# A fused filter, bidirectional scan and FFN block: VectorE's side steps put on odd scans

## The chip, the cores and the metric

The kernel runs on one core of one Trainium2 chip. The metric is device microseconds of one execution, from launch to end; lower is better. Engines are named as in the profile: PE (TensorE matmuls, PEld its weight loads), DVE (VectorE), ACT (ScalarE), POOL (GpSimd) and SP (which issues the DMAs).

## The reference, cut to what matters

Eight images of 64 channels and 128 x 128 pixels go through two layers, all in float32.

1. **Filter.** A 3x3 convolution to 32 channels, a leaky ReLU and a 1x1 convolution give nine logits for each pixel. Their softmax is a low-pass kernel of that pixel; the output is `x + high`, where `high` sums nine shifted copies of x, each times (delta - softmax).
2. **Two bidirectional scans** (state space blocks) over the 16384 pixels of an image as one sequence. In short, for each direction and layer:

```
xc = silu(causal_conv1d(x));  dt = softplus(linear(xc));  B, C = linear(xc)
h[d,n,t] = exp(dt[d,t] * A[d,n]) * h[d,n,t-1] + dt[d,t] * B[n,t] * xc[d,t]      # 128 channels x 16 states
y[d,t]   = (sum over n of h[d,n,t] * C[n,t] + D[d] * xc[d,t]) * silu(z[d,t])
```

3. **Mix and FFN.** `x + dw * x_mamba`, where both factors are 3x3 convolutions (one per channel), then a layer norm, an FFN with a 3x3 convolution of 2 x 170 channels, gelu(g1) * g2, a projection and a residual sum.

## The kernel before, in words

**The scan is the backbone.** An image's sequence is cut into 16 time chunks of T = 1024, and it is walked four times (two layers, two directions), so an image has 64 chunks and the program 512. The channel-state pairs of a chunk (128 x 16 = 2048) fill 16 tiles of 128 partitions, so a chunk is **16 scans**, numbered u = 0 to 15 here, and the program has 8192 scans. Two neighbouring scans are a *pair* k (u = 2k and 2k+1). In each layer the second walk (`second`) also multiplies by the gate on DVE (`y_out`, L1272) and norms the result (`normed`, L1303); in the first walk ACT copies y out instead.

**One scan** is:
- `drive` (L1191, POOL, for a pair, written five scans ahead): bu = dt*x times B.
- `decay` (L1199, ACT, issued two scans ahead): w = exp(dt * A) into one of two PSUM tiles `w`.
- `scan` (L1218 or L1220, DVE): h = w*h + bu along time.
- `product` (L1235 DVE, L1237/L1239 POOL): h times C. For even u other than 4 and 12 it is POOL's (except in the scan after an FFN's gelu); then the scan writes to SBUF and its `w` tile is free when the scan ends. For odd u, and u = 4 and 12, it is DVE's own: the scan writes back into `w`, and that tile is free only when DVE's product has read it.
- `keep` (L1242, ACT): copies the last state for the next chunk.
- `collect` (L1257, PE): for a pair, sums over states into PSUM `y`.

**A chunk's preparation** runs beside the chunks before it: `conv` (L1066, PE, xp) and `conv_out` (L1072, ACT, xc) at u = 7 and 8, `gate` and `gate_out` (L1081, L1089) at 9 and 10, `silu` (L1092, ACT, with two table loads) at 11, `step`/`step_out` (L1108, L1115) at 14 and 15, `softplus` (L1121, ACT, with two table loads) at 2, `dtx` (L1147, POOL) at 5, and, for second walks, `project` (op, L1286), `residual` (L1292) and `square` (L1299) at 5 and 6.

**Beside the scans run the other layers of the next or the last image**, as tiles of 8 image rows: the *front* (filter, two layer norms, a root-mean-square norm; one tile each 24 scans), the *mix* (each 13) and the *FFN* (each 24). Seen from the start of an image's 1024 scans, the last image's mix takes about scan 0 to 174, its FFN 178 to 562, the next image's front 569 to 1010. Some tiles of the first and the last image run by other plans (`plan_alone`, and the `alone` branch of the FFN), which the change leaves as they are.

**What sets the order.** Nothing is left to a scheduler: `at(time, phase, function)` puts each step at a scan number and at one of seven phases within that scan, and the steps are written out in the order of (time, phase), within a phase in the order in which they were planned (chunks before tiles, older tiles before younger ones). Each engine then runs its own instructions strictly in that order.

```
    FEED, SCAN, MID, PROD, EXP, DECAY, REST = range(7)
            if u % 2 or u % 8 == 4 or self.t0 + u - 1 in gelu_times:
                return False
            return True
                at(b + u - 2, EXP, self.decay, u)
                at(b + u, SCAN, self.scan, u)
```

So DVE's side steps (`less_max`, `sums`, `weighted`, `scaled`, `third_norm` of the front, `times` and `scaled` of the mix, `rest_times` and `times` of the FFN), which are in phase MID, stand between that scan and, on odd u, DVE's own product. On an even u whose product is POOL's they stand between two scans. Steps of ACT's side are in DECAY, behind that scan's `keep` and `decay`; PE's, POOL's and SP's are in REST.

**Names that the change touches.** Front, with a = its start and b = a - 24: `logits` (lp, L547/L548), `less_max` (mx and lg, L554/L556), `exps` (L559, ACT), `sums` (sm, L563/L564), `softmax` (L567, POOL), three `piece` (sp, L571, ACT) and two `less_piece` (L575, POOL), `turn` (L580, PE) and `turned` (L584, ACT), nine `weight` (wb, L594, PE), `weighted` (t, L598, DVE) and `gather` (acc, L609, PE), `scaled` (hc, L629), `first_norm` (L633), `pointwise_out` (dwt, L642), `third_norm` (hn, L664). Mix: `times` (dwv, L820), `plus` (x, L823, POOL). FFN: `times` (ga, L961), `project` (fo, L972 to L977, PE), `add` (L983, ACT). Front tiles start alternately at u = 1 and u = 9 of a chunk, FFN tiles at u = 2 and u = 10; with 24 scans to a tile the pattern comes again every 48 scans, or three chunks. PSUM has one bank `bg`, one `acc`, one `mm` (xp, zp, dp, op) and one `y`.

## Time and profile before

| what | value |
|---|---|
| median of 3 runs | 28420.1 us (28417.24, 28420.1, 28466.43) |
| the profiled execution's own time | 28448.51 us |
| its span, first to last instruction | 28446.7 us |
| granted TensorE clock, mean | 0.881 |
| DVE busy | 26999.1 us (95%), 17438 instructions |
| POOL busy | 26718.7 us (94%), 8092 instructions |
| PE, ACT busy | 22906.5 us (81%), 18789.5 us (66%) |
| one DVE scan, one DVE product | 2343 ns, 1222 ns |
| one `drive`, one product on POOL | 4553 ns, about 2375 ns |
| `decay` on ACT | 1118 ns |

An engine's busy share is an average over stages. The table of windows and the timeline, which the prediction shows, tell which engine sets the pace in which stage; the view of waits names for each idle time the instruction that ended it. The profiled execution lies 28.4 us above the median of the three runs, inside their spread.

### The profile page before, as it was taken

Reading aid. Unit: us, or ns where it says so; the run is one execution under the profiler, and the core shown is the slowest. Engines: PE = TensorE matmul, PEld = TensorE weight load, DVE = VectorE, ACT = ScalarE, POOL = GpSimd, SP = SyncE. Lnnn points to the kernel's source line nnn. Section 1 sums busy time; section 2 is a strip of 40 time slices with the busy share of each in tenths; the row PEclk is TensorE's granted clock in tenths of the full one; section 3 lists DMA queues with packets and bytes.
Section 4 is the critical chain, followed back from the end, with each engine's and each line's share of the span. In section 5 each row is a group of like instructions: output and inputs, shape, how many; then the busy total and the mean of one; then the engine's idle time right before and its main releaser. Section 6 shows DMA issues by size and latency. Waiting matters only on the chain. (4 is left out here: it accounts for less than half of the span.)

```text
span 28446.7 us, 310539 instructions
## 1 busy us (share of the span) xinstructions
PE 22906.5 (81%) x97708; PEld 7249.4 (25%) x97708; DVE 26999.1 (95%) x17438; ACT 18789.5 (66%) x29130; POOL 26718.7 (94%) x8092
## 2 busy tenths in 40 slices
PE   7667888878888787888878788787887878888678
PEld 3212322223222232222322222222222222222123
DVE  6999999999999999999999999999999999999997
ACT  4666666666666666666666666666666666666663
POOL 4999999999999999999999999999999999999993
PEclk8777889988899888988889888898888988889789
DMA  6777787777877778777777777777777777777674
GB/s 163 233 243 226 239 259 244 243 231 237 263 245 241 228 241 262 241 241 230 246 256 242 239 232 248 254 246 235 234 252 246 250 229 239 255 244 248 209 257 138
DMA packets 2592492, 6762.70 MB, mean 238 GB/s; under 512 B 431494, under 2 KB 737046, under 8 KB 2589686
## 3 DMA queue, kind: packets, MB, share of 16 engines
q1 hardware_dynamic: 2589958, 6742.69, 73.0%
q8 instruction: 772, 12.65, 0.2%
q14 instruction: 882, 7.23, 0.1%
q10 hardware_dynamic: 880, 0.14, 0.0%
HBM read 5509.49 MB, written 1265.19 MB: 238 GB/s over the span
## 5 line engine op out<-in xcount | busy, mean ns | idle before, releaser
L1191 POOL TENSOR_TENSOR bu<-dup,bp 128x2048 f32<-128x2048 f32 x4096 | 18612.8, 4553 | 37.2 <-DMA bp<-bc_dram 17.9
L1199 ACT ACTIVATE w<-dtp,a_neg 128x1024 f32<-128x1024 f32 x8192 | 9162.7, 1118 | 1488.3 <-DVE hs L1220 657.6
L1235 DVE TENSOR_TENSOR hs<-w,cp 128x1024 f32<-128x1024 f32 x5232 | 6393.1, 1222 | 269.3 <-DMA cp<-bc_dram 99.1
L1220 DVE TENSOR_TENSOR_SCAN w<-w,state,bu 128x1024 f32<-128x1024 f32 x2651 | 6212.1, 2343 | 155.2 <-ACT w L1199 126.0
L1218 DVE TENSOR_TENSOR_SCAN w<-w,state,bu 128x1024 f32<-128x1024 f32 x2581 | 6048.4, 2343 | 95.8 <-ACT w L1199 75.1
L1257 PE MATMUL y<-hs,sel_y 128*32 128x512 f32 x32768 | 4996.0, 688 | 748.9 <-POOL hs L1239 434.2
L1242 ACT COPY state<-w 128x1 f32<-128x1 f32 x5232 | 828.5, 158 | 5315.9 <-DVE hs L1235 5253.4
L1237 POOL TENSOR_TENSOR hs<-hs,cp 128x1024 f32<-128x1024 f32 x1515 | 3609.4, 2382 | 332.8 <-DVE hs L1218 217.6
L1239 POOL TENSOR_TENSOR hs<-hs,cp 128x1024 f32<-128x1024 f32 x1445 | 3423.4, 2369 | 423.8 <-DVE hs L1220 299.4
L1218 DVE TENSOR_TENSOR_SCAN hs<-w,state,bu 128x1024 f32<-128x1024 f32 x1515 | 3550.2, 2343 | 155.3 <-ACT state L1242 74.5
L1220 DVE TENSOR_TENSOR_SCAN hs<-w,state,bu 128x1024 f32<-128x1024 f32 x1445 | 3384.5, 2342 | 97.9 <-ACT state L1242 61.9
L1066 PE MATMUL xp<-hn,wx 128*128 128x512 f32 x4096 | 2459.4, 731 | 1036.6 <-ACT xc L1072 434.2
L897 PE MATMUL fp<-fw,bgw 128*128 128x512 f32 (+1 forms) x5760 | 2166.7, 622 | 166.3 <-DMA fw<-xn_dram 166.0
L1108 PE MATMUL dp<-xc,wdt 128*128 128x512 f32 x2048 | 1356.2, 749 | 635.6 <-ACT dt L1115 305.9
L1257 PEld LDWEIGHTS y<-hs,sel_y 128*32 128x32 f32 x32768 | 720.6, 114 | 4456.2 <-issue 2557.1
L1250 PE MATMUL y<-xc,dskip 128*64 128x512 f32 x4096 | 1381.2, 759 | 404.4 <-ACT yv L1274 302.5
L1072 ACT ACTIVATE xc<-xp,cbias 128x512 f32<-128x512 f32 x1024 | 701.3, 685 | 1195.0 <-PE xp L1066 1191.0
L1066 PEld LDWEIGHTS xp<-hn,wx 128*128 128x128 f32 x4096 | 839.6, 224 | 2524.4 <-issue 1033.7
L68 ACT ACT_TABLE_LOAD x1137 | 1458.8, 1283 | 21.3 <-PEq L1429 0.7
L903 PE MATMUL fp<-fw,bgw 64*128 64x512 f32 (+1 forms) x5760 | 1385.7, 608 | 0.0
L609 PE MATMUL acc<-t,ident 128*128 128x512 f32 x2160 | 1307.1, 693 | 0.0
L594 PE MATMUL wb<-wt,sel_k 65*128 65x512 bf16 x1152 | 509.4, 443 | 979.6 <-DVE t L598 975.5
(212 smaller groups left out, 25989.6 us busy)
## 6 DMA issues: line engine op xcount, KB each, us to landing
bp<-bc_dram SPq DMA_DIRECT2D x4096, 256.0 KB, 4.0
dup<-du_dram SPq DMA_DIRECT2D x4096, 256.0 KB, 5.2
dtp<-dt_dram SPq DMA_DIRECT2D x4096, 256.0 KB, 5.1
cp<-bc_dram SPq DMA_DIRECT2D x4096, 256.0 KB, 4.8
hn<-hn_dram SPq DMA_DIRECT2D x1024, 256.5 KB, 4.4
dt_dram<-dt SPq DMA_DIRECT2D x512, 512.0 KB, 3.0
du_dram<-du SPq DMA_DIRECT2D x512, 512.0 KB, 2.6
yf_dram<-yv SPq DMA_DIRECT2D x512, 256.0 KB, 3.3
```

What stands on the lines that cost most here:

```text
L68: nc.scalar.preload_act_table_set("natural_log_exp_and_others")
L897: nc.tensor.matmul(o, wpair[:, i, g, m], self.win[h][:, i : i + ROWS, 0:W], start=(i == 0), stop=False)
L903: nc.tensor.matmul(o, wlast[rows, i, g, m], self.win[h][rows, i : i + ROWS, lo : W + lo], start=False, stop=(i == 2),)
L1066: nc.tensor.matmul(self.xp[h], wx[:, self.l, self.d, i, :], self.hn2[:, s.start + 2 * i : s.stop + 2 * i], start=(i == 0), stop=(i == 1),)
L1191: nc.gpsimd.tensor_tensor(bu, self.dup[self.pairs[k][1]], self.over_pair("bp", k), ALU.mult)
L1199: nc.scalar.activation(w, self.dtp[gp][:, i, :], AF.Exp, scale=a_neg[:, self.l, self.d, g, j : j + 1])
L1218: nc.vector.tensor_tensor_scan(to, w, bu, s0, ALU.mult, ALU.add)
L1220: nc.vector.tensor_tensor_scan(to[:, ::-1], w[:, ::-1], bu[:, ::-1], s0, ALU.mult, ALU.add)
L1235: nc.vector.tensor_tensor(out, hs, c, ALU.mult)
L1237: nc.gpsimd.tensor_tensor(out, hs, c, ALU.mult)
L1239: nc.gpsimd.tensor_tensor(out[:, ::-1], hs[:, ::-1], c[:, ::-1], ALU.mult)
L1257: nc.tensor.matmul(self.y[lo : lo + 32, :], sel_y, hs[:, i, s], start=False, stop=(k % 4 == 3))
```

## The change

All edits are to the numbers of the plan; no instruction is added or taken away.

- **Front.** `less_max` goes from scan a - 1 to a (and from phase DECAY to MID), `exps` with it; `sums` and `softmax` from a + 1 to a + 2; the pieces, `turn` and `turned` one scan later; `gather` one later; both `scaled` and all that hangs on them (`first_norm`, `pointwise`, `pointwise_out`, the second centring, `second_norm`, the stores) one later; `third_norm` from a + 55 to a + 56. As a is odd, all of DVE's moved steps go from even to odd scans. The nine `weighted` stay.
- **Mix.** `times`, `plus`, `scaled` and `norm` go to the next odd scan where they were on an even one.
- **FFN.** The two `times` of a tile go from one even scan (a + 20) to the odd ones at a + 19 and a + 21; `load_x2`, `project`, `add` and the store go one scan later.
- **Scan.** `collect` of the pairs k = 1 and k = 5 goes one scan later (u = 6 and 14).
- One `load_hn` (that of chunk 14) goes one scan later.

```diff
-            at(b + 23, DECAY, self.less_max)
-            at(b + 23, DECAY, self.exps)
-            at(b + 25, MID, self.sums)
-            at(b + 25, REST, self.softmax)
+            at(a, MID, self.less_max)
+            at(a, DECAY, self.exps)
+            at(a + 2, MID, self.sums)
+            at(a + 2, REST, self.softmax)
             for i in range(3):
-                at(b + 26 + 2 * i, DECAY, self.piece, i)
+                at(a + 3 + 2 * i, DECAY, self.piece, i)
                 if i < 2:
-                    at(b + 27 + 2 * i, REST, self.less_piece, i)
-            at(b + 31, REST, self.turn)
-            at(b + 32, DECAY, self.turned)
+                    at(a + 4 + 2 * i, REST, self.less_piece, i)
+            at(a + 8, REST, self.turn)
+            at(a + 9, DECAY, self.turned)
...
-                at(t + 13, REST, self.gather, k)
+                at(a + k + 14, REST, self.gather, k)
...
-            at(a + 29, MID, self.scaled, n1)
-            at(a + 29, DECAY, self.first_norm)
-            at(a + 30, REST, self.pointwise)
-            at(a + 31, DECAY, self.pointwise_out)
+            at(a + 30, MID, self.scaled, n1)
+            at(a + 30, DECAY, self.first_norm)
+            at(a + 31, REST, self.pointwise)
+            at(a + 32, DECAY, self.pointwise_out)
...
-            at(a + 37, MID, self.scaled, n2)
-            at(a + 37, DECAY, self.second_norm)
-            at(a + 37, REST, self.store_h)
-            late, end = (a + 46, a + 55) if self.c < NCH - 1 else (a + 37, a + 43)
+            at(a + 38, MID, self.scaled, n2)
+            at(a + 38, DECAY, self.second_norm)
+            at(a + 38, REST, self.store_h)
+            late, end = (a + 46, a + 56) if self.c < NCH - 1 else (a + 38, a + 44)
...
-            at(a + 8, MID, self.times)
-            at(a + 8, REST, self.plus)
+            at(a + 8 | 1, MID, self.times)
+            at(a + 8 | 1, REST, self.plus)
...
-            at(a + 17, MID, self.scaled, n1)
+            at(a + 17 | 1, MID, self.scaled, n1)
...
-                groups = ((0, 0, self.first_out, 5), (6, 2, None, 0), (14, 1, self.times, 20))
-                gelus, out = GELU, 20
+                groups = ((0, 0, self.first_out, 5), (6, 2, None, 0), (14, 1, self.times, 19))
+                gelus, out = GELU, 21
...
-                    at(a + to, MID if end == self.times else DECAY, end, h)
+                    late = 0 if self.alone or end == self.first_out else 2 * h
+                    at(a + to + late, MID if end == self.times else DECAY, end, h)
...
-            at(b + (5 if self.i == NCH - 2 else 3), REST, self.load_hn)
+            at(b + (6 if self.i == NCH - 2 else 3), REST, self.load_hn)
...
-                at(b + 2 * k + 3 + (k % 4 == 0), REST, self.collect, k)
+                at(b + 2 * k + 3 + (k % 4 < 2), REST, self.collect, k)
```

More of the change, by code (lines that the diff above doesn't have):

```diff
@@ L678, in plan @@
             at(b + 21, REST, self.logits)
-            at(b + 23, DECAY, self.less_max)
-            at(b + 23, DECAY, self.exps)
-            at(b + 25, MID, self.sums)
-            at(b + 25, REST, self.softmax)
+            at(a, MID, self.less_max)
+            at(a, DECAY, self.exps)
+            at(a + 2, MID, self.sums)
+            at(a + 2, REST, self.softmax)
             for i in range(3):
-                at(b + 26 + 2 * i, DECAY, self.piece, i)
+                at(a + 3 + 2 * i, DECAY, self.piece, i)
                 if i < 2:
-                    at(b + 27 + 2 * i, REST, self.less_piece, i)
-            at(b + 31, REST, self.turn)
-            at(b + 32, DECAY, self.turned)
+                    at(a + 4 + 2 * i, REST, self.less_piece, i)
+            at(a + 8, REST, self.turn)
+            at(a + 9, DECAY, self.turned)
             at(a + 6, REST, self.load_xb)
             for k in range(9):
-                t = a + k
-                at(t + 11, DECAY, self.weight, k)
-                at(t + 12, MID, self.weighted, k)
-                at(t + 13, REST, self.gather, k)
+                at(a + k + 11, DECAY, self.weight, k)
+                at(a + k + 12, MID, self.weighted, k)
+                at(a + k + 14, REST, self.gather, k)
             at(a + 23, DECAY, self.filtered)
@@ L702, in plan @@
             at(a + 27, REST, n1.spread, bg_tile)
-            at(a + 29, MID, self.scaled, n1)
-            at(a + 29, DECAY, self.first_norm)
-            at(a + 30, REST, self.pointwise)
-            at(a + 31, DECAY, self.pointwise_out)
-            at(a + 31, REST, self.store_rows, dw_img[self.p], "dwt")
-            at(a + 31, REST, self.centered, acc_tile, "xn")
-            at(a + 32, DECAY, self.centered_out)
-            at(a + 33, REST, lambda: n2.means(acc_tile, self.sq))
-            at(a + 34, DECAY, n2.means_out)
-            at(a + 35, REST, n2.spread, acc_tile)
-            at(a + 37, MID, self.scaled, n2)
-            at(a + 37, DECAY, self.second_norm)
-            at(a + 37, REST, self.store_h)
-            late, end = (a + 46, a + 55) if self.c < NCH - 1 else (a + 37, a + 43)
+            at(a + 30, MID, self.scaled, n1)
+            at(a + 30, DECAY, self.first_norm)
+            at(a + 31, REST, self.pointwise)
+            at(a + 32, DECAY, self.pointwise_out)
+            at(a + 32, REST, self.store_rows, dw_img[self.p], "dwt")
+            at(a + 32, REST, self.centered, acc_tile, "xn")
+            at(a + 33, DECAY, self.centered_out)
+            at(a + 34, REST, lambda: n2.means(acc_tile, self.sq))
+            at(a + 35, DECAY, n2.means_out)
+            at(a + 36, REST, n2.spread, acc_tile)
+            at(a + 38, MID, self.scaled, n2)
+            at(a + 38, DECAY, self.second_norm)
+            at(a + 38, REST, self.store_h)
+            late, end = (a + 46, a + 56) if self.c < NCH - 1 else (a + 38, a + 44)
             at(late, DECAY, self.third_square)
@@ L850, in plan @@
             at(a + 15, REST, n1.spread, bg_tile)
-            at(a + 17, MID, self.scaled, n1)
-            at(a + 17, DECAY, self.norm)
-            at(a + 17, REST, self.store_rows, xn_img, "hc")
+            at(a + 17 | 1, MID, self.scaled, n1)
+            at(a + 17 | 1, DECAY, self.norm)
+            at(a + 17 | 1, REST, self.store_rows, xn_img, "hc")
     def plan_mix(b, a, step):
```

## The prediction, made before the changed kernel had run

> **What bounds the kernel now.** I read the page first (DVE 95% busy, POOL 94%), then the windows by stage, then DVE's waits, then timelines of single chunks; the order of both programs' instructions shows what moves where. Below, four windows in the middle of the run: mix and early FFN, late FFN, and the front in first and in second walks. Columns: window, busy us of PE, PEld, DVE, ACT, POOL, granted clock, DMA share, GB/s.

> ```profile
> 7298.60:8140.30 841.70, 666.04 (x2842) 181.30 (x2840) 802.28 (x460) 560.13 (x840) 841.70 (x251) 0.89 0.79 254
> 8140.30:9004.80 864.50, 758.40 (x3155) 236.39 (x3151) 832.71 (x507) 592.43 (x880) 813.66 (x231) 0.96 0.74 246
> 9261.50:9855.20 593.70, 461.97 (x2009) 150.87 (x2009) 582.42 (x401) 403.00 (x653) 584.76 (x192) 0.86 0.69 227
> 9855.20:10623.30 768.10, 650.18 (x2965) 238.42 (x2963) 740.51 (x529) 529.78 (x873) 710.63 (x227) 0.88 0.73 236
> ```

> In the first window POOL is busy for all of its 841.70 us: POOL sets the pace for the first quarter of each image, and what DVE saves there buys nothing. In the others DVE is idle for 11 to 32 us and POOL for 9 to 57: DVE sets the pace, less its stalls. So the change can win two things: cheaper side steps, and fewer stalls.

> **Term 1: a side step is cheaper on an odd scan.** DVE's timeline in a front chunk:

> ```profile
> 10143.77 2.34 DVE L1218 TENSOR_TENSOR_SCAN hs<-w,state,bu 128x1024 f32<-128x1024 f32 x1
> 10146.03 0.66 DVE L598 TENSOR_TENSOR t<-xb,wb 128x512 f32<-128x512 f32 x1
> 10146.61 2.35 DVE L1218 TENSOR_TENSOR_SCAN w<-w,state,bu 128x1024 f32<-128x1024 f32 x1
> ...
> 10155.76 2.35 DVE L1218 TENSOR_TENSOR_SCAN w<-w,state,bu 128x1024 f32<-128x1024 f32 x1
> 10158.02 0.67 DVE L598 TENSOR_TENSOR t<-xb,wb 128x512 f32<-128x512 f32 x1
> 10158.61 1.21 DVE L1235 TENSOR_TENSOR hs<-w,cp 128x1024 f32<-128x1024 f32 x1
> 10159.73 2.34 DVE L1218 TENSOR_TENSOR_SCAN hs<-w,state,bu 128x1024 f32<-128x1024 f32 x1
> 10161.99 2.33 DVE L1218 TENSOR_TENSOR_SCAN w<-w,state,bu 128x1024 f32<-128x1024 f32 x1
> 10164.35 1.23 DVE L1235 TENSOR_TENSOR hs<-w,cp 128x1024 f32<-128x1024 f32 x1
> 10165.50 2.34 DVE L1218 TENSOR_TENSOR_SCAN hs<-w,state,bu 128x1024 f32<-128x1024 f32 x1
> ```

> From start to start, an even scan takes 2.26 us bare (10159.73 to 10161.99) and 2.84 with a side step (10143.77 to 10146.61): 0.58 for the step. An odd scan with its product takes 3.51 bare (10161.99 to 10165.50) and 3.97 with a step in between (10155.76 to 10159.73): 0.46. Independent instructions overlap by some 0.08 us, while the product that needs its scan starts 0.03 after the scan's end; a side step fills that hole. Saved: 0.12 us for each step that stood alone and stands alone again. [...] The 2.36 us (scan to its product) against 2.26 (scan to an independent step) above show a difference here, and I follow the rows.

> - Front, 120 tiles (7 x 16 + 8): three lone groups each (mx with lg, the first hc, hn) go to odd scans where nothing stands: 360 x 0.12 = 43 us. The second hc stands beside a t before and after: 0. sm falls beside yv in second walks, and in first walks just ahead of a scan that waits for softplus: 0. Half of the mx groups (60) fall in chunks whose scans 10 and 11 wait for ACT anyhow: minus 7. Left: 36.
> - FFN, 112 tiles: two steps in one even scan (2 x 0.58) become two lone ones (2 x 0.46): 0.24 x 112 = 27; the first fifth of the FFN lies in POOL's stretch: 21.
> - Mix: POOL's stretch, 0; at most some 125 steps x 0.12 = 15.

> **Term 2: a stall filled in the FFN.** In the second walk, chunk type 1 (chunk number mod 3), scan 14 waits 0.43 us for ACT, behind silu (30 times in six images, 13.0 us), and both `times` stand behind it. With the first at scan 13 the wait shrinks by its 0.43: x 6 x 7 images = 18 us.

> **Term 3: PE's order in the FFN.** The largest single stall of DVE in the FFN:

> ```profile
> 8432.91 1.98 PE L972 MATMUL fo<-ga,bgw 128*64 128x512 f32 x4
> ...
> 8437.95 1.98 PE L1066 MATMUL xp<-hn,wx 128*128 128x512 f32 x4
> 8439.98 0.69 ACT L1072 ACTIVATE xc<-xp,cbias 128x512 f32<-128x512 f32 x1 [4.88 <-PE xp L1066]
> ...
> 8442.38 2.36 DVE L1220 TENSOR_TENSOR_SCAN w<-w,state,bu 128x1024 f32<-128x1024 f32 x1 [2.67 <-ACT w L1199]
> ```

> The FFN's projection (fo, 4.1 us here) stands between the two halves of xp; ACT waits 4.88 us for the second half with the next `decay` behind it, and scan 11 starts 2.67 us late. This is so in chunk type 0 of second walks, 18 times in six images, 49.7 us. With `project` one scan later, fo stands behind the second xp in PE's order. That xp could start once xc's first half is out (8433.74) and, at the 3.78 us that the first half took at half clock, end at 8437.6; xc then ends at 8438.3 and `decay` at 8439.7, against 8439.63 as scan 11's earliest start: no stall. 49.7 x 7/6 = 58 us; I take 50, since fo now stands ahead of zp, and ACT's gate copy can cost up to 0.4 us in each of the 21 chunks. Bounds 0 and 58.

> **Term 4: ACT's steps ahead of silu (u = 11) in the front.** Scan 14 there waits 62 us in six images. One sp cast (0.23 us; chunk type 2) and one pair of r steps (0.26 + 0.21; type 1) go from 11 to 12, behind the `decay` that is late: 0.23 x 8 x 7 = 13 and 0.42 x 4 x 7 = 12. Of these 25 I take 20; bounds 0 and 25.

> **Term 5, a cost: ACT's steps ahead of softplus (u = 2).** `pointwise_out` (0.68 us) goes from u = 0 to u = 1 in chunk type 0, into ACT's unbroken run from `keep` to `decay(5)`. In first walks scan 5 has 0.03 us to spare there (median): 0.65 x 3 x 7 = 14 us lost. In second walks 1.3 us to spare hides it; without that cover 24 more (bounds 0 and 38).

> **Term 6, a cost: POOL's order.** POOL's timeline at the first front tile of an image:

> ```profile
> 5814.96 0.30 POOL L567 TENSOR_TENSOR lg<-lg,sm 128x72 f32<-128x72 f32 x1
> 5815.22 2.35 POOL L1239 TENSOR_TENSOR hs<-hs,cp 128x1024 f32<-128x1024 f32 x1
> 5817.54 4.54 POOL L1191 TENSOR_TENSOR bu<-dup,bp 128x2048 f32<-128x2048 f32 x1
> ```

> `softmax` now comes behind this product and `drive`: 5821.8 to 5822.1. ACT's first sp cast, one scan later than before, then stands in front of `keep` and `decay` of scan 7, which is done at 5823.7; scan 7 started at 5822.63 and would start 0.23 earlier now: 1.3 us lost. `less_piece` comes behind dtx and one more `drive`, at 5829.2; the next cast, with hidden_out's 1.3 us behind it, delays scan 9 by 2.8. Together about 4.2 us an image, 29 for seven. Stalls let POOL catch up: at scan 6 it starts its product 7 to 8 us behind the scan's end here, but 3.1 in the median first-walk chunk and at most 2.6 in second walks, and the cast hurts only from about 3 us on. I take 30; bounds 0 and 60.

> **Term 7: lp.** mx waits for PE at u = 8 (28.8 us in six images, 34 in seven), and one scan later it won't. But that PE queue (project, lp, xp) holds ACT, too: scans 10 and 11 there wait 52 us, and the time would reappear there, or at sm, which now waits for `exps` behind a gate copy. I take 0; bounds minus 20 and plus 34.

> **At nothing.** The third norm's means (PE) now wait for lg of one scan later, as both use bank bg: about 2.5 us of PE's queue once a tile, hidden because ACT reaches the result 1.5 us after it is done; uncovered, some 1 us x 100. POOL's waits for sm and sp (41 and 71 us in the front) vanish: POOL has room there. `gather` and `collect` one later free PE of waits for POOL (62 us in the front) and are needed by nothing sooner. The next FFN tile's first matmul finds bank bg free one scan after `add` is due, not two: its result is due five scans later. SP's queue moves with its producers: loads lead their use by two scans or more.

> **Sum.** 36 + 21 + 18 + 50 + 20 - 14 - 30 + 0 = 101 us. Against the profiled execution's own 28448.5 us: 28347. The median of the runs is 28420, so this is 0.26% below it; 0.2%, about 57 us, is what a measurement of this kernel can tell from no change (28363 and 28477).

> **Rivals.**
> 1. *Slower: POOL's order decides in every front tile.* Without term 6 the sum is 131 us; over 120 front tiles a stall of 1.1 us each takes all of it, and from 1.6 us on the kernel is slower. For it: in first walks POOL's lag of 3.1 us is just at the margin, and cheaper side steps in the same stretch (u = 1 to 9) raise it. Against: second walks, and that a stall cures the lag. At 2 us each: 28448.5 - 131 + 240 = 28557.
> 2. *No change: the stalls move.* ACT and PE are in order, and what one chunk's scan 11 gains another wait takes back (term 3 at half or less, 4 at nothing, 5 and 6 as above): 36 + 21 + 0 + 12 - 14 - 30 = 25, so 28424.
> 3. *The change doesn't do what it says.* The order listing shows the steps ahead of the products and fo behind xp: excluded.

> **Chances and range.** The forecast (a gain beyond 57 us) 0.62, no change 0.20, slower 0.18. All terms at their best: 43 + 42 + 18 + 58 + 25 + 34 = 220, 28228; three runs reach 31 us below the profiled execution, so I go to 28215. At the worst bounds (half of term 3, no 2 and 4, 14 + 60 + 20 lost): 12 us over the old, 28460; a part of the slower rival takes it to 28490.

> **What would show it.** Right: odd scans with a lone step at 3.97 us; fo behind the second xp and no wait near 2.7 us at scan 11; DVE's busy time as before and its idle time some 60 to 100 us smaller. Wrong: ACT waiting for lg on POOL for several us, with DVE waiting for `decay` at scans 7 and 9; waits for sm on ACT; POOL's idle time growing in the first quarter of an image.

## The result, and the profile after

The changed kernel takes 28604.8 us (median of 6 runs, 28584.99 to 28622.85) against 28421.8 us for the kernel before (6 runs beside it): a ratio of 1.0060, 95% interval 1.0050 to 1.0071. By the ratio it is about 170 us slower (the two medians lie 183 us apart), where 101 us less were forecast. Its profiled execution took 28590.2 us, with a span of 28588.4 us.

Busy time by engine, from the top of the page of the changed kernel:

```profile
span 28588.4 us, 310543 instructions
PE 23060.4 (81%) x97708; PEld 7247.1 (25%) x97708; DVE 26930.1 (94%) x17438; ACT 18772.1 (66%) x29130; POOL 26719.2 (93%) x8092
```

DVE is busy 69 us less than before (26999.1), with the same number of instructions: the cheaper side steps are there. But the span grew by 142 us, so DVE is idle for some 211 us more. PE is busy 154 us *more* (22906.5 before) for the same 97708 matmuls, and the mean granted clock fell from 0.881 to 0.874. They ran slower; hold on to that.

The same four windows as in the prediction, cut at the same scans of the same image (us; busy PE, PEld, DVE, ACT, POOL; granted clock, DMA share, GB/s):

```profile
7389.10:8234.20 845.10, 666.75 (x2847) 181.85 (x2846) 800.45 (x460) 558.98 (x840) 843.53 (x252) 0.88 0.78 251
8234.20:9077.70 843.50, 742.06 (x3154) 228.52 (x3150) 828.84 (x506) 594.40 (x880) 811.00 (x230) 0.98 0.76 253
9333.80:9936.90 603.10, 472.25 (x1989) 154.16 (x1991) 579.99 (x402) 400.90 (x652) 584.74 (x191) 0.83 0.68 223
9936.90:10718.90 782.00, 671.73 (x2987) 244.57 (x2980) 738.55 (x529) 528.26 (x872) 710.80 (x228) 0.86 0.71 232
```

The late FFN takes 843.5 us instead of 864.5. Both front windows grew, 593.7 to 603.1 and 768.1 to 782.0, though DVE is busy 2 us less in each, and the granted clock in them fell from 0.86 to 0.83 and from 0.88 to 0.86. Over the whole run, from scan to scan, the FFN of seven images (scans 176 to 592) gains 109 us. The front of seven (592 to 984) loses 169, image 0's front 35, and the 216 scans between front and FFN, with the front's last steps and the mix, lose 30. These are single executions. A stage that no edit touches differs by some 30 us from one profile to another (the FFN of the kernel with S alone, below), so smaller differences of a stage show little.

What DVE waited for (waits of DVE; us in total, times, longest):

```profile
DVE w L1217 <- ACT w L1198: 240.2, 202, 2.5
DVE hs L1217 <- ACT w L1198: 171.7, 113, 8.0
DVE w L1219 <- ACT w L1198: 159.8, 125, 2.8
```

Before, these three read:

```profile
DVE w L1218 <- ACT w L1199: 75.1, 105, 2.3
DVE hs L1218 <- ACT w L1199: 70.0, 47, 3.0
DVE w L1220 <- ACT w L1199: 126.0, 96, 2.8
```

Scans that wait for `decay` on ACT account for 300 us of new waiting, more than the whole 211. Of the other waits some grew (`normed` for its spread by 33 us, `times` of the FFN by 27) and some fell. Adding up DVE's idle time ahead of scans, products, `t` and `mx` by chunk type (six images, as in the prediction), front stalls went from 206 to 381 us. Where they stand is in the table below.

Terms 1 and 3 are to be seen as forecast. DVE's timeline in a front chunk, with a lone `hc` on an odd scan:

```profile
10278.36 2.35 DVE L1217 TENSOR_TENSOR_SCAN hs<-w,state,bu 128x1024 f32<-128x1024 f32 x1 [0.85 <-ACT w L1198]
10280.62 2.33 DVE L1217 TENSOR_TENSOR_SCAN w<-w,state,bu 128x1024 f32<-128x1024 f32 x1
10282.86 0.67 DVE L629 TENSOR_TENSOR hc<-hc,rb 128x512 f32<-128x512 f32 x1
10283.45 1.21 DVE L1234 TENSOR_TENSOR hs<-w,cp 128x1024 f32<-128x1024 f32 x1
10284.58 2.34 DVE L1217 TENSOR_TENSOR_SCAN hs<-w,state,bu 128x1024 f32<-128x1024 f32 x1
```

From 10280.62 to 10284.58 it is 3.96 us, where 3.97 was expected. In the FFN, the chunk that answers to the one shown before:

```profile
8525.46 1.98 PE L1065 MATMUL xp<-hn,wx 128*128 128x512 f32 x4
8527.37 1.08 PE L970 MATMUL fo<-ga,bgw 128*64 128x512 f32 x4
8527.48 0.69 ACT L1071 ACTIVATE xc<-xp,cbias 128x512 f32<-128x512 f32 x1 [1.41 <-PE xp L1065]
...
8530.59 2.33 DVE L1219 TENSOR_TENSOR_SCAN w<-w,state,bu 128x1024 f32<-128x1024 f32 x1
```

`fo` stands behind the second xp, ACT waits 1.41 instead of 4.88 us, and scan 11 starts without a wait.

### The profile page after: what moved, and what is told of

The parts are those of the page before. It is cut to its first block, busy times and chain, and to the rows that moved or that the text cites. A ratio compares the mean times of both kernels' runs of the same rounds, so it can differ in the third digit from the quotient of the medians.

```text
span 28588.4 us, 310543 instructions
## 1 busy us (share of the span) xinstructions
PE 23060.4 (81%) x97708; PEld 7247.1 (25%) x97708; DVE 26930.1 (94%) x17438; ACT 18772.1 (66%) x29130; POOL 26719.2 (93%) x8092
## 5 line engine op out<-in xcount | busy, mean ns | idle before, releaser
L1256 PE MATMUL y<-hs,sel_y 128*32 128x512 f32 x32768 | 5059.5, 693 | 378.8 <-POOL hs L1238 311.7
```

What stands on the lines that cost most here:

```text
L1256: nc.tensor.matmul(self.y[lo : lo + 32, :], sel_y, hs[:, i, s], start=False, stop=(k % 4 == 3))
```

## The experiments

The change falls into parts that can be put in or taken out alone: F, the FFN's two edits; S, the softmax chain (mx to `turned`) a scan later; N, the two norm chains, pointwise and gather a scan later; C, the sums over states of pairs 1 and 5 a scan later. Each kernel was compared with the kernel before on the same chip; a ratio of 0.001 is 28 us. The mix's moves were not tried alone: over scans 0 to 176 of seven images the nine kernels with them are -1 to 14 us longer than the kernel before, the six others -1 to 9, so no effect of theirs can be seen.

### One part back, or one part alone

**F alone.** The kernel before with these lines of the diff, shortened:

```
-  (14, 1, self.times, 20))        gelus, out = GELU, 20
+  (14, 1, self.times, 19))        gelus, out = GELU, 21
+  late = 0 if self.alone or end == self.first_out else 2 * h
```

> The kernel before with the FFN's edits alone (times at 19 and 21, project and add one scan later). Theory A (the prediction's FFN terms hold, the loss is made elsewhere): terms 1, 2 and 3 of the FFN give 21 + 18 + 50 = 89 us less than the kernel before, about 28331; scan 11 of chunk type 0 in second walks no longer waits 49.7 us in six images. Rival B (the FFN's edits are part of the loss, because fo now holds zp or the wait at ga grows): 28420 or more.

Measured: 0.9984 (0.9976 to 0.9993), 45 us faster. Theory A in direction, half in size (see term 2 below). The loss is elsewhere.

**One part taken out of the changed kernel**: C (`(k % 4 < 2)` back to `(k % 4 == 0)`), S (the lines mx to `turned` back to `b + 23` ... `b + 32`), N (`a + 30` ... `a + 38` back to `a + 29` ... `a + 37`, `end` to `a + 55`, gather to `a + k + 13`).

> The changed kernel with only the sums over states put back (pairs 1 and 5 of each chunk at scans 5 and 13 again). Theory C: in the front those matmuls, a scan later, stand on PE ahead of the second dp (asked for at scan 15) and of op and xp (scans 5 to 8), so that bc comes 1 to 2 us later and decay(3) with it; putting them back gives most of the 38 us of scan 3's waits and a part of those at scans 10 and 11: 60 to 100 us less than the changed kernel's 28605. Rival D (the loss is from the front's own steps): within 25 us of 28605.

> The changed kernel with only the softmax chain of the front (mx, lg, exps, sums, softmax, pieces, turn) put back one scan earlier. Theory S: exps behind the gate copy and sm waiting for it on DVE in chunk type 2, POOL's softmax behind drive, and the casts behind POOL are the loss at scans 7, 9, 10 and 11: the waits there shrink by 29 + 66 - 29 (mx waits again) us in six images, so some 80 us less than 28605. Rival D2 (norm chain or sums over states): within 25 us of 28605.

> The changed kernel with the front's two norm chains (with pointwise, the third norm's end) and gather put back one scan earlier. Theory N: second_norm at scan 15 behind the second dt and pointwise_out at scan 1 ahead of softplus lie in ACT's unbroken stretch up to decay(5), and cost the waits of scans 3 and 5 (0 to 38 us and 10 to 43 us in six images, before and after): 70 to 100 us less than 28605, even though term 1's 0.12 us a step for two of three lone groups (24 us) is given up. Rival D3 (it is the softmax chain or the sums over states): 28605 or a little more.

Measured: C back 1.0023 (1.0013 to 1.0033), S back 1.0017 (1.0008 to 1.0026), N back 1.0006 (0.9997 to 1.0015). Against the 1.0060 of the change, the parts put back return 105, 122 and 154 us. All three gave back more than their theories said (60 to 100, some 80, 70 to 100), and together they would return 381 us of a loss of 216 (171 plus the 45 of F). The parts are not independent.

**One part put into the kernel before**, nothing else:

> The kernel before with only pairs 1 and 5 of each chunk's sums over states a scan later. Theory I (shared slack: each part is hidden while the other two stand where they were, so the costs do more than add): within 30 us of the kernel before, since the FFN wins some 35 us by it (84 against 50 in its late part with and without) and the front loses about 25 to 45. Rival J (each part costs what its undoing gave back): some 90 us slower than before.

> The kernel before with only the softmax chain of the front (mx to turn) one scan later. Theory I: 30 to 50 us slower: the 29 us of mx's wait at scan 8 reappear at scan 10, and POOL's late softmax and pieces cost about 28 us in six images at scans 7, 9 and 11 of chunk type 1. Rival J: some 110 us slower. The prediction's terms 1, 6 and 7 for this part alone: 36/3 + 0 - 30, so about 18 us slower.

> The kernel before with only the front's norm chains, pointwise, third norm's end and gather one scan later (and the one load of hn that has to follow). Theory I: 50 to 80 us slower, from scan 5 of chunk type 0 (term 5 of the prediction, there minus 14), scan 3 of type 1 and scan 11 of type 2. Rival J: some 140 us slower. The prediction's own terms for this part: 24 (two of three lone groups) + 12 - 14, so 20 us faster.

Measured: C 1.0017 (1.0008 to 1.0025), S 1.0013 (1.0004 to 1.0022), N 1.0017 (1.0008 to 1.0026): 48, 37 and 48 us slower. With F's -45 that adds up to 88 us; the change costs 171. In size theory I holds for S and, just below its range, for N; C was expected within 30 us and is at 48, and its profile places it where the theory did (front 55 us longer, FFN 26 shorter). For S and N the profiles do not: their steady front stretches are as long as before (0 and -3 us), and S alone shows 34 us in the FFN, none of whose steps it moves. Where S and N alone lose their time is thus not shown. All parts together lose 169 us in the front. So the question became: what is harmless there alone and costs when two come together?

### Where the parts meet: PE's order and its clock

The stalls of DVE in the front, us in six images ("type" is the chunk number mod 3, counted from the start of the image):

| place | before | change | C back | S back | N back | gather | turn | filler | PE order |
|---|---|---|---|---|---|---|---|---|---|
| scan 5, type 0 | 2 | 33 | 33 | 22 | 2 | 30 | 31 | 26 | 31 |
| t at scans 8, 9, type 0 | 34 | 30 | 0 | 47 | 62 | 66 | 45 | 41 | 0 |
| scan 3, type 1 | 0 | 38 | 16 | 12 | 0 | 2 | 32 | 19 | 0 |
| scans 7, 9, 11, type 1, first walks | 0 | 29 | 31 | 0 | 28 | 32 | 31 | 28 | 29 |
| scans 13, 14, type 1, second walks | 10 | 37 | 51 | 0 | 10 | 49 | 10 | 18 | 10 |
| mx, scans 10, 11, type 2, second walks | 81 | 117 | 124 | 84 | 94 | 104 | 106 | 113 | 98 |
| scan 11, type 2, first walks | 10 | 40 | 31 | 16 | 20 | 14 | 37 | 43 | 8 |
| all ahead of scans, products, `t`, `mx` | 206 | 381 | 347 | 267 | 273 | 353 | 355 | 359 | 236 |

(The last row leaves out the waits of `sm`: 39 us with S back, some 11 in the others, 2 before.)

Scans 13 and 14 show the meeting most clearly: 10 us or less without S or without N, 37 to 51 with both (the change, C back, gather). Here is one such chunk of the changed kernel (timeline of PE, ACT and DVE; in brackets the idle time before and who ended it):

```profile
10552.07 0.69 ACT L642 ACTIVATE dwt<-dwp,v_dw_b 128x512 f32<-128x512 f32 x1
...
10552.81 2.07 PE L621 MATMUL cp<-hc,center 128*128 128x512 f32 x2 [1.77 <-ACT dwt L642]
...
10554.81 0.63 PE L580 MATMUL tp<-identb,sp 128*54 128x128 bf16 x4
...
10555.37 1.97 PE L1080 MATMUL zp<-hn,wz 64*64 64x512 f32 x4
...
10557.38 0.58 ACT L1088 COPY gate<-zp 128x512 f32<-128x512 f32 x1 [3.62 <-PE zp L1080]
...
10566.76 2.35 DVE L1217 TENSOR_TENSOR_SCAN hs<-w,state,bu 128x1024 f32<-128x1024 f32 x1 [1.88 <-ACT w L1198]
```

N makes `dwt` 3.2 us later, and cp waits for it. S moves the transposes tp, which stood ahead of cp, behind it, so PE idles 1.77 us. With S back, tp stands ahead and the same chunk reads:

```profile
10509.58 0.38 PE L580 MATMUL tp<-identb,sp 128*54 128x128 bf16 x4
...
10513.24 1.12 PE L621 MATMUL cp<-hc,center 128*128 128x512 f32 x2 [1.27 <-ACT dwt L642]
```

In the changed kernel cp takes 2.07 us for its two passes, and zp, which ACT needs for the gate, is late. The windows of this kernel around it show why (the column before the DMA share is the granted clock):

```profile
10549.20:10552.80 3.60, 1.84 (x12) 0.16 (x8) 3.60 (x3) 2.51 (x6) 3.60 (x2) 0.97 0.99 349
10552.80:10556.20 3.40, 3.39 (x8) 1.17 (x10) 3.40 (x3) 0.96 (x1) 3.40 (x2) 0.50 0.55 138
```

The clock halves (0.97 to 0.50) just as cp starts. There are 30 such chunks in six images, and in 24 of them PE waits for `dwt`. With N and not S, PE idles 1.27 us there and cp always runs at full speed; with both, 1.77 us, and in 11 of the 24 chunks cp runs wholly or partly at half clock (19 with C back, 18 with gather back, whose stalls in the table are the larger for it). The changed kernel's own chunks tell the clock from the order: scans 13 and 14 wait 2.42 us a chunk in those 11, 0.79 in the other 13, and 0.42 before. Two kernels test this: one puts only the transposes back ahead of cp, the other adds a matmul that nobody reads.

```
-  at(a + 8, REST, self.turn)
+  at(a + 7, REST, self.turn)
```

> The changed kernel with only the front's transposes (turn, to tp) one scan earlier, so that they stand on PE ahead of cp of the norm chain and not behind it. Theory W (PE's clock: in chunk type 1 of second walks cp waits for pointwise_out anyway; without tp ahead of it PE is idle for 1.77 instead of 1.27 us of a 3.41 us stretch, drops to half clock, and cp, tp and the second zp take twice as long): cp at 0.70 again instead of 0.88 on average, the second zp about 1 us earlier (10.4 instead of 11.4 us after scan 8), scans 13 and 14 waiting about 10 instead of 37 us in six images; 20 to 50 us less than the changed kernel. Rival X (the lateness of the norm chain on ACT alone delays silu): no change in those waits, within 15 us of the changed kernel.

```
+  def fill(self):
+      fl = bg_tile("fl")
+      nc.tensor.matmul(fl, center, wx[:, 0].rearrange("p d i c -> p (d i c)"), start=True, stop=True)
...
+  at(a + 32, REST, self.fill)
   at(a + 32, REST, self.centered, acc_tile, "xn")
```

> The changed kernel with one matmul more for each front tile (128x512, into bank bg, read by nobody) ahead of cp of the norm chain, in PE's wait for pointwise_out; nothing else moves. Theory W: the matmul costs PE nothing, since it runs while cp would wait, and keeps PE busy for 1 us more of that stretch, so that cp runs at 0.70 and the second zp about 0.5 to 1 us earlier; scans 13 and 14 of chunk type 1 in second walks wait 10 to 20 instead of 37 us in six images, and PE's granted clock in the front rises: 0 to 30 us less than the changed kernel, although PE has 120 x 1 us more to do. Rival X (it is the order alone: tp and zp behind a late cp): the waits stay and the kernel is 0 to 60 us slower than the changed one.

Measured: turn 1.0040 (1.0027 to 1.0053), filler 1.0039 (1.0026 to 1.0052), 57 and 60 us less than the change (its interval 1.0050 to 1.0071 just touches theirs). The same chunk with the filler:

```profile
10542.42 1.12 PE L625 MATMUL fl<-wx,center 128*128 128x512 f32 x2
...
10544.25 1.13 PE L621 MATMUL cp<-hc,center 128*128 128x512 f32 x2 [0.70 <-ACT dwt L646]
...
10545.64 1.08 PE L1085 MATMUL zp<-hn,wz 64*64 64x512 f32 x4
...
10546.76 0.58 ACT L1093 COPY gate<-zp 128x512 f32<-128x512 f32 x1 [1.56 <-PE zp L1085]
...
10556.14 2.35 DVE L1222 TENSOR_TENSOR_SCAN hs<-w,state,bu 128x1024 f32<-128x1024 f32 x1 [0.75 <-ACT w L1203]
```

cp takes 1.13 us instead of 2.07 and is never at half clock in the 24 chunks; ACT waits 1.56 instead of 3.62; scan 14 waits 0.75 instead of 1.88. A useless matmul makes this kernel faster. Theory W holds at this place; rival X, that order alone decides, falls here: tp is still behind cp. At full clock scans 13 and 14 still wait 0.75 us a chunk, against 0.42 before: that much is the order's. The gains of 57 and 60 us are above what was expected (20 to 50, 0 to 30); the profiles show 26 and 24 us of them in the front, and the rest is not placed. Neither removes the stalls elsewhere.

**Gather** back to one scan behind its product (all taps but the first): `self.gather` at `a + k + 13 + (k == 0)`.

> The changed kernel with only gather's PE matmuls of taps 1 to 8 put back to one scan behind their product on DVE (tap 0 stays two scans behind). Theory G: a tap's sum a scan later stands on PE between the two halves of xp (chunk type 2, scan 8) and ahead of bcp (scan 0), so xc's second half, decay(11) and decay(3) come late: putting it back gives the 49 us of scan 11 in second walks down to about 25, and scan 3's 26 down to about 10, in six images: 40 to 70 us less than the changed kernel. Rival H (the norm chain's own ACT steps do it): within 20 us of the changed kernel, and those waits stay.

Measured: 1.0040 (1.0028 to 1.0053), 57 us less than the change. The changed kernel's timeline in chunk type 2 shows what it does:

```profile
10259.55 0.69 ACT L1071 ACTIVATE xc<-xp,cbias 128x512 f32<-128x512 f32 x1 [4.87 <-PE xp L1065]
...
10260.43 1.12 PE L609 MATMUL acc<-t,ident 128*128 128x512 f32 x2
...
10261.40 1.88 PE L1065 MATMUL xp<-hn,wx 128*128 128x512 f32 x4
...
10263.31 0.69 ACT L1071 ACTIVATE xc<-xp,cbias 128x512 f32<-128x512 f32 x1 [1.55 <-PE xp L1065]
...
10265.72 2.36 DVE L1217 TENSOR_TENSOR_SCAN w<-w,state,bu 128x1024 f32<-128x1024 f32 x1 [1.51 <-ACT w L1198]
```

The last tap's sum (acc) stands between the two halves of xp: ACT waits 1.55 us and scan 11 1.51. On average, in second walks, the last pass of the second xp starts 10.32 us after scan 8 with it and 9.75 without (9.38 before); bcp starts 5.95 and 4.13 us after scan 0 in 24 chunks of type 1 (3.91 before). Theory G holds: scan 3 to 2 us, scan 11 from 49 to 33 (25 expected). But t at scans 8 and 9 now waits 66. The sums over states act on the same wait: with C back, that bcp starts at 5.16 us, and scan 3 waits 16 instead of 38.

**The norm chain kept tight**: `scaled` and `first_norm` stay on the odd scan, pointwise to spread go back to where they were before.

> The changed kernel with scaled and first_norm still at the odd scan, but pointwise on PE in that same scan, so that pointwise_out, centered and the second norm's means and spread are back where they stood before the change. Theory N2 (what costs is pointwise_out and centered one scan later, not the step on DVE): scan 5 of chunk type 0 waits about 5 instead of 33 us in six images, scans 13 and 14 of type 1 in second walks about 10 instead of 37, while the lone steps stay cheap: 70 to 120 us less than the changed kernel. Rival Y (gather, sums over states and softmax carry the loss): within 40 us of the changed kernel.

Measured: 1.0034 (1.0021 to 1.0046), 74 us less than the change. Scan 5 falls from 33 to 7 us and scans 13, 14 to 13, as theory N2 says; but scan 11 of type 1 in first walks rises from 4 to 42, and the profile's front outside image 0 is as long as before the edit. One stall was traded for another there; what its profile gains (54 us) lies in image 0's front and in the stretch between front and FFN, 27 us each.

**PE's three pure moves undone beside the front, and only these.** Every step of DVE, ACT and POOL stays where the change puts it, and so do PE's steps inside the norm chains, `gather` of tap 0 and, away from the front, the sums over states:

```
-  at(a + 8, REST, self.turn)
+  at(a + 7, REST, self.turn)
-  at(a + k + 14, REST, self.gather, k)
+  at(a + k + 13 + (k == 0), REST, self.gather, k)
-  at(b + 2 * k + 3 + (k % 4 < 2), REST, self.collect, k)
+  at(b + 2 * k + 3 + (k % 4 == 0 or (k % 4 == 1 and not self.beside_front)), REST, self.collect, k)
```

> The changed kernel with its three pure moves on PE undone beside the front, and nothing else: the transposes (turn) ahead of cp, gather of taps 1 to 8 one scan behind its product, and the sums over states where they were in chunks beside a front (a scan later elsewhere). Every step of DVE, ACT and POOL stays as the change puts it. Theory P (the loss is PE's order and the clock that follows from it): by the single undoings the front loses 27 + 35 + 47 us less, image 0's front some 20 less; some 28440, within 40 us of the kernel before, with scan 3 of chunk type 1, scan 11 of type 2 and scans 13 and 14 near their values of before. What stays is POOL's late softmax (scans 7, 9 and 11, about 28 us in six images) and pointwise_out ahead of softplus (scan 5, about 25). Rival Q (ACT's and POOL's later steps carry it): 28530 or more.

Measured: 28378.3 us, 0.9980 (0.9971 to 0.9989): 228 us less than the change and 57 less than the kernel before. Its front windows, at the same scans:

```profile
9262.40:9859.40 597.00, 472.49 (x1995) 152.37 (x1989) 579.57 (x401) 401.94 (x652) 585.03 (x191) 0.83 0.69 226
9859.40:10623.10 763.70, 657.52 (x2981) 242.96 (x2977) 736.88 (x530) 528.63 (x873) 710.55 (x228) 0.88 0.72 237
```

The second walk takes 763.7 us, less than the 768.1 before. Theory P holds, and gave too little (28440): three edits that touch nothing but PE's order turn a loss of 171 us into a gain of 57. The column "PE order" shows what stays, as expected: scan 5, and scans 7, 9, 11. Rival Q falls.

**The parts that win, together.** The first kernel is F with C only in chunks that lie beside no front; the second adds the first norm's `scaled`, `first_norm` and the third norm on odd scans.

> The kernel before with the FFN's edits and the sums over states a scan later only in chunks that lie beside no front. Theory E (a sum over states a scan later lets the FFN's matmuls through sooner and costs only where the front's matmuls stand behind it): late FFN 78 us shorter in the profile as in the combined kernel, not 48 as with the FFN's edits alone; 65 to 90 us less than the kernel before. Rival Z: 45 us less, as with the FFN's edits alone.

> The kernel before with the FFN's edits, the sums over states a scan later only in chunks that lie beside no front, the first norm's scaled and first_norm at odd scans with everything that follows where it was, and the third norm at an odd scan. By the parts: 45 (FFN's edits alone) + 35 (sums over states in the FFN) + 2 x 14 (two lone groups of 0.12 us in 120 tiles), so some 100 us less than the kernel before, 28320 to 28350. Rival Z (the parts do not add, as the front's did not): 0 to 50 us less than the kernel before.

Measured: 0.9985 (0.9976 to 0.9995) and 0.9981 (0.9972 to 0.9990). Neither differs from F alone (0.9984): rival Z in the first; in the second 54 us faster, at the edge of what rival Z gave. In time the sums over states a scan later add nothing to F (known to within some 28 us), although the profile of the changed kernel had hinted at 35 us. The waits do differ: at scans 10 and 11 of type 1 in the FFN's second walks, `yv` included, they are 27 to 52 us in the eleven kernels with the later sums and 63 to 84 in the five without. The change with PE's order undone is as fast as the best of these.

## Why the prediction was wrong

The step that failed is the paragraph **at nothing**: "`gather` and `collect` one later free PE of waits for POOL (62 us in the front) and are needed by nothing sooner." Both halves are true (PE's waits for POOL fell to 21 us in the front) and beside the point. Those who read the matmuls of these three moves lost little (in the whole run `yv` waits 130 us for `y`, 106 before, `wt` 4.0 us for tp in both, and ACT's copy of acc none for acc). The loss is with those that now find one directly ahead of them: bcp (5.95 us after scan 0, 4.13 with gather back) and the second xp (its last pass 10.32 us after scan 8, 9.75 with gather back), for which ACT waits with `decay` in its queue. `turn`, the third, was not costed at all; its move left PE idle ahead of cp (1.77 us, 1.27 with S back). I had used this very reading as a gain for `fo` in term 3, and not as a cost for three other moves on the same queue. In sum these three moves cost 228 us; without them the change gains 57, within its range.

By the terms (times from the profiles; six images, or seven where said):

- **Term 1** (57): right. DVE's busy time fell by 69 us, and a lone step takes 3.96 us with its scan and product where 3.97 was expected.
- **Term 2** (18): wrong in sign. The wait at scan 14 went, 13.0 to 0, but the first `times`, at scan 13, now waits for its matmuls (fp), 22.8 us in 24 chunks. In seven images it is 11 lost.
- **Term 3** (50): right. 49.7 us went; 4.4 came back at yv.
- **Term 4** (20): the part of type 2 was larger than its 13 (scan 14 lost 23 us of its waits, 27 in seven images). The part of type 1 has the wrong sign: that chunk's waits rose from 10 to 37, where S and N meet. With N alone they fell to 0, as the term had it.
- **Term 5** (-14): mis-sized. Scan 5 of type 0 waits 33 us, 31 more than before, 36 in seven images, near the bound of 38. The cover in second walks gave way too.
- **Term 6** (-30): right, in mechanism and size. At the first front tile of an image:

```profile
5882.43 0.25 ACT L571 CAST sp<-lg 128x72 bf16<-128x72 f32 x1 [5.38 <-POOL lg L567]
5889.48 0.25 ACT L571 CAST sp<-lg 128x72 bf16<-128x72 f32 x1 [4.56 <-POOL lg L575]
```

  ACT waits for POOL, and scans 7, 9 and 11 lose 28.9 us in six images, 34 in seven.
- **Term 7** (0): right as far as it went. mx's 28.8 us went and scan 10's waits rose by 30.8. The 35 us more at scan 11 are mostly PE's order (26 instead of 49 us with PE's moves undone).
- **The bank bg**: this wait I did name, and it is small in the steady front (at most 0.7 us, in nine chunks of all). In image 0's front, where the tiles begin at other scans of a chunk, the means wait 4 to 6 us for lg once a tile: 32 us there, 16 before. That front is 35 us longer, and still 19 with PE's moves undone. But with N put back the means still wait 26 us there and that front is only 5 us longer than before, so this wait is not the most of it.
- **Rivals**: the slower one had the right sign and nearly the right time (28557) by the wrong mechanism; POOL's order cost what term 6 says and no more. The loss came nearest to the second, stalls that move, with a sign it had not been given.

## What to carry to other kernels

Cost each move on an in-order queue for the instructions that come to stand directly behind it and for those that it no longer stands ahead of, on every engine that it touches; "nobody needs it sooner" says nothing about who now stands behind it. Try the moves of each engine as separate kernels: three parts that cost 37 to 48 us each alone (133 in sum) cost 216 together, the mix's moves included. When an engine's busy time grows with the same instructions, as PE's did by 154 us here, look at its clock (0.881 to 0.874).
